# One quarter of M made of 12-bit parts, and a softmax maximum issued ahead of the next rows' parts

## The chip, the cores and the metric

The kernel runs on one core of a Trainium2 chip. The metric is the device time of one execution in microseconds (us), as the median of several runs. Engines are named as the profile names them: PE (TensorE, matmuls), PEld (its weight loads), DVE (VectorE), ACT (ScalarE), POOL (GpSimd) and SP (SyncE). DVE, ACT and POOL each work through one queue of instructions in order; SP and POOL also issue the transfers (DMAs).

## The reference

One decoder layer on x of 4 batches x 512 rows x 512 columns, in float32. The change touches the first of its three blocks, self-attention with 16 heads of 128:

```python
q = x @ Wq + bq ; k = x @ Wk + bk ; v = x @ Wv + bv      # x here: layernorm of the rows
att = softmax(q @ k / sqrt(128))                          # per head: 128 x 128, contracted over the 512 rows
x   = x + (att @ v) @ Wo + bo
x   = x + gamma * cross(layernorm(x), ctx)                # cross-attention, 8 heads
x   = x + ffn(layernorm(x))                               # ternary weights, silu gate
```

## The kernel before, in words

**Work.** The 16 heads go in four quarters j = 0..3 of four heads (512 columns). With the Gram matrix G of the normalized rows of a batch (tiles `xn`, bank `pg`, L444), each quarter of each batch is this chain of 512x512 products: U from the rows and Wo (bank `pu`, tiles `u`), Y from G and Wk (`py`, `y`), M from Wv and U (`pm`, `m`), the scores from Wq and Y (`sc`, L523), a softmax of the scores (maximum `nmax` L531, its scaling L534, exponential on ACT L538, division by the sum L549, result `e`), then, one quarter later, the transpose of `e` (`pe`, L126) and the output product (`po`, L562), which DVE adds to the accumulators `acc` (L564).

**Two kinds of product.** `products_f32` (L384) is 16 float32 matmuls, each of which the profile records as two; ACT copies the four results out. `products` makes the same of parts of 12 bits: each operand is a triple h, l, d. For a pair of result tiles there are 16 matmuls h.h and l.l (L350, L351) into two banks, which ACT copies to tiles of the pool `t` (L357, three buffers), then 8 matmuls d.d (L362) into two other banks; DVE adds both (`total`, L372). Two pairs make one product. `tri_of` makes the parts of a tile: h on ACT (L188), l and d on DVE (L189, L190).

**Which kind where.** Batches 1 to 3 use parts throughout. In batch 0 the weights are loaded raw, and `FIRST` says from which quarter on a product uses parts: 1 for U and Y, 4 (`HG`, so never) for M. `exact(n, b, j)` asks this.

**Weights of batch 0.** `first_weights` loads four raw chunks per weight by SP. For q, k and v it also loads a row `last` by SP, and a bias row into the last line of chunk 3 by a POOL DMA (L265), and DVE folds the two into each chunk (L269). Chunk 3, the one with the bias, is loaded first. `keep_weights` then makes the parts (h on ACT L306, l on DVE L308, and d on DVE only where the quarter is exact) and stores them to DRAM by POOL DMAs (L288), where later batches load them. A part that was not made, batch 1 makes (`weights`, d on DVE L336, stored by POOL L339).

**Order.** PE, DVE and ACT instructions are placed by a scheduler when the kernel is built; `tc.issue_after(mark)` holds a group back until a named instruction has been placed. `mark["copied"]` is the last copy out of a `products` call, `mark["nmax"]` the last softmax maximum. In quarter 3 of batch 0, `normed(1, xs, ...)` normalizes the rows of batch 1 (statistics on DVE L95 and L96, square root on ACT L103, reciprocal L112, four normalizations L120, four one-column memsets L407), and `parts_of(1, xs)` makes their parts (tiles `xh`, `xl`, `xd`). Before a tile that came by DMA is used, `settle` multiplies it by a one (L603, L610) that is made of the newest copied tile (`recent`), which ties it to that point of the order.

**What follows quarter 3 of batch 0.** The Gram matrix of batch 1 (`pg`), the transpose `pe` and output `po` of quarter 3 in its midst, and then quarter 0 of batch 1. Beside batch 1 run as side steps the row norms of batch 0 for the cross-attention (`row_norms`: square root `std_c` on ACT, reciprocal and copy on DVE L112 and L686, a store `norm_a` and two loads `norms` by POOL, L687 and L690), the cross-attention itself (`qs`, `kh` on ACT L723 and L727, `xs` on PE L740), and the bias additions to the new accumulators, which POOL computes (L872).

Of the kernel before, what the change touches and what calls it, by code (L numbers as in the profile page):

```python
# [11 lines left out]
F32 = mybir.dt.float32  # L12

F32R = mybir.dt.float32r
# [5 lines left out]
P = 128  # L20
# [4 lines left out]
NG, HG = 4, 4  # L25
# [14 lines left out]
def decoder_layer_kernel(  # L40
# [169 lines left out]

    FIRST = {"o": 1, "k": 1, "v": HG}

    def exact(n, b, j):
        return b > 0 or j >= FIRST[n]

# [9 lines left out]
    last_rows = {}  # L227

    def last_tile(n, j):
        return first[0].tile([P, GW], F32, tag="last", bufs=3, name=f"{n}_last_{j}")  # L230

    def first_last_rows():

# [38 lines left out]
    def keep_weights(n, j, chunks, first, gate):  # L272


        def part(p, k):
            name = f"{n}_{p}_{j}_{k}"
            if n == "o" and exact(n, 0, j):
                if p != "d":
                    return u3p.tile([P, D], F32R, tag="u3", name=name)
                pool, tag, bufs = first[0], "od", 4  # L280
            elif n == "v":
                pool, tag, bufs = first[0], "vpart", 6
            else:
                pool, tag, bufs = first[1], "part", 12
            return pool.tile([P, GW], F32R, tag=tag, bufs=bufs, name=name)

        def keep(name, tile):
            nc.gpsimd.dma_start(name[ts(k, P), :], tile)  # L288

        def behind(n, k):  # L290

            if n == "v" and "copied" in mark:
                return tc.issue_after(mark["copied"])
            if n == "k" and k >= KC // 2 and "nmax" in mark:
                return tc.issue_after(mark["nmax"])
            return nullcontext()

        tris = []
        for k, t in enumerate(chunks):
            if n == "q":  # L300
                keep(kept_q[j], t)
                continue
            tri = Tri(part("h", k), part("l", k), part("d", k) if exact(n, 0, j) else None)
            h, l = tri.h.bitcast(F32), tri.l.bitcast(F32)
            with behind(n, k):
                nc.scalar.mul(tri.h, t, gate[0])  # L306
                keep(kept[n, j, "h"], h)
                nc.vector.scalar_tensor_tensor(tri.l, h, -S, t, ALU.mult, ALU.add)  # L308
                keep(kept[n, j, "l"], l)
                if tri.d is not None:  # L310
                    nc.vector.tensor_tensor(tri.d, l, h, ALU.subtract)
                    keep(kept[n, j, "d"], tri.d.bitcast(F32))
            tris.append(tri)
        return tris
# [28 lines left out]
    def products(name, lhs, rhs, done, tick):  # L343

        for pair in ((0, 1), (2, 3)):
            ph = {i: bank(f"{name}h_{i}") for i in pair}
            for k in range(4):
                for i in pair:
                    a, c = lhs(k, i), rhs(k)
                    nc.tensor.matmul(ph[i], lhsT=a.h, rhs=c.h, start=(k == 0), stop=False)  # L350
                    nc.tensor.matmul(ph[i], lhsT=a.l, rhs=c.l, start=False, stop=(k == 3))  # L351
                if k == 1:
                    tick()
            hs = {}
            for i in pair:
                hs[i] = tp.tile([P, 512], F32, tag="t", name=f"{name}t_{i}")
                mark["copied"] = nc.scalar.copy(hs[i], ph[i]).ins  # L357
            tick()
            pd = {i: bank(f"{name}d_{i}") for i in pair}
            for k in range(4):  # L360
                for i in pair:
                    nc.tensor.matmul(  # L362
                        pd[i], lhsT=lhs(k, i).d, rhs=rhs(k).d, start=(k == 0), stop=(k == 3)
                    )
            for i in pair:
                done(i, hs[i], pd[i])
            recent[:] = [recent[-1], hs[pair[0]]] if recent else [hs[pair[0]]]
            tick()
# [8 lines left out]
    def products_f32(name, lhs, rhs, done, midway=None):  # L377

        for i in range(4):
            if i == 2 and midway:  # L380
                midway()
            p = bank(f"{name}_{i}")
            for k in range(4):
                nc.tensor.matmul(  # L384
                    p, lhsT=lhs(k)[:, ts(i, P)], rhs=rhs(k), start=(k == 0), stop=(k == 3)
                )
            done(i, p)
# [11 lines left out]
    def normed(b, xs, by_chunk):  # L399

        mv = small.tile([P, NG, 2], F32, tag="mv", name=f"mv_a_{b}")

        def finish(part, std):
            rstd = inverse(std, f"a_{b}_{part[0]}")
            for g in part:
                normalize(xs[g], xs[g], mv[:, g, 0:1], rstd[:, g - part[0] : g - part[0] + 1])
                last = nc.vector.memset(xs[g][:, D - 1 : D], 1.0).ins  # L407
            return last

        parts = [(g,) for g in range(NG)] if by_chunk else [tuple(range(NG))]  # L410
        due = []
        for part in parts:
            for g in part:
                if b > 0:
                    settle(xs[g])
                moments(mv[:, g, :], xs[g], f"a_{b}_{g}")
            if b == 0:
                with tc.issue_after(mark["std"]):
                    nc.scalar.copy(accs[part[0]], xs[part[0]])
            due.append((part, std_of(mv[:, part[0] : part[-1] + 1, :], f"a_{b}_{part[0]}")))  # L420
            if len(due) > 1:
                finish(*due.pop(0))
        return finish(*due.pop())
# [457 lines left out]
    for j in range(HG):  # L881
        us, ys, ms = {}, {}, {}

        def to(tiles, pool, tag, name):
            def done(i, p, d=None):
                tiles[i] = pool.tile([P, 512], F32, tag=tag, name=f"{name}_{i}")
                if d is None:
                    evict(tiles[i], p)
                else:
                    total(tiles[i], p, d)  # L890

            return done

        ticks = [0]

        def third_tick():
            ticks[0] += 1
            if ticks[0] == 3:
                midway()

        def midway():
            if waiting:
                waiting[2] = turned(*waiting[:3])

        w = first_weights("o", j, first, gates["o"])
        if exact("o", 0, j):
            w = keep_weights("o", j, w, first, gates["o"])
            products(
                f"pu_0_{j}", lambda c, m: cols(x3[c], m), lambda c: w[c],
                to(us, u3p, "u3", f"u_0_{j}"), lambda: None,  # L910
            )
        else:
            products_f32(
                f"pu_0_{j}", lambda c: xs[c], lambda c: w[c], to(us, u3p, "u3", f"u_0_{j}")
            )
            if j == 0:
                g3 = gram_rest(0, G)
            with tc.issue_after(rows_done):
                keep_weights("o", j, w, first, gates["o"])
        gates["v"] = gate_of(us[3])  # L920
        w = first_weights("k", j, first, gates["k"])
        done = to(ys, yp, "y", f"y_0_{j}")
        if exact("k", 0, j):
            w = keep_weights("k", j, w, first, gates["k"])
            products(
                f"py_0_{j}", lambda e, m: cols(g3[e], m), lambda e: w[e], done, third_tick
            )
        else:
            products_f32(f"py_0_{j}", lambda e: G[e], lambda e: w[e], done, midway)
            keep_weights("k", j, w, first, gates["k"])  # L930
        gates["o"] = gates["k"] = gates["q"] = gate_of(ys[3])
        if waiting:
            output(*waiting)
        w = first_weights("v", j, first, gates["v"])
        products_f32(f"pm_0_{j}", lambda k: w[k], lambda k: us[k], to(ms, mp, "m", f"m_0_{j}"))
        keep_weights("v", j, w, first, gates["v"])
        w = first_weights("q", j, first, gates["q"])
        e = scores(0, j, w, ys)
        keep_weights("q", j, w, first, gates["q"])
        if j == 0:  # L940
            bo_bc = bias_rows(0)
            load(gam, gamma.to_broadcast([P, 1]))
            biased(accs, bo_bc)
        if j + 1 == FIRST["o"]:
            x3 = parts_of(0, xs)
        if j == HG - 2:
            xs = rows_of(1)
        if j == HG - 1:
            normed(1, xs, False)
            x3 = parts_of(1, xs)  # L950
        waiting = [0, j, e, ms, accs]
    first_pools.close()

# [233 lines left out]
```

## Time and profile before

| | |
|---|---|
| median of 3 runs | 1158.3 us (1157.48 to 1159.26) |
| profiled execution | 1157.7 us; its span in the trace 1155.9 us, so 1.8 us lie around it |
| PE busy | 1144.6 us, 99% of the span |
| DVE, ACT, POOL busy | 818.9 us (71%), 524.5 us (45%), 318.8 us (28%) |
| granted TensorE clock | 9 tenths or more in every slice |
| DMA | 270.16 MB, mean 234 GB/s; 9 tenths busy in many slices of the first half |

Rows of a timeline give the start in the span, the duration, the engine, line, operation, output<-input, the count that the row gathers, and in brackets the idle time before it with what ended it. Durations of neighbouring records of one engine overlap a little, so a distance from start to start is what one more instruction costs.

### The profile page before, as it was taken

The page shows a single profiled execution, that of the slowest core. Times are in us where ns is not written, and L with a number is a line of the kernel's source. Part 1 is how long each engine was busy: PE and PEld are TensorE (multiplying, and loading weights), DVE is VectorE, ACT ScalarE, POOL GpSimd, SP SyncE. Part 2 cuts the span into 40 slices and gives each one's busy share as a digit, 9 for nine tenths or more (in the row PEclk, how much of TensorE's full clock was granted, in tenths as well). Part 3 has the DMA queues.
Part 4 walks back from the last instruction along what each step waited for, and adds up shares of the span by engine and source line. Part 5 has one row for each costly group of instructions (what it writes and reads, how often), then busy time and mean ns, then how long its engine had stood idle before and what let it go on. Part 6 is the DMA issues. An engine that isn't in the chain of part 4 may idle for free.

```text
span 1155.9 us, 16616 instructions
## 1 busy us (share of the span) xinstructions
PE 1144.6 (99%) x5282; PEld 856.5 (74%) x5282; DVE 818.9 (71%) x1802; ACT 524.5 (45%) x1073; POOL 318.8 (28%) x550
## 2 busy tenths in 40 slices
PE   8999999999999999999999999999999999999998
PEld 4486684777777768887786787777778877777886
DVE  6768657979797967869697758787957857536232
ACT  5434334435445443545354434544455768534020
POOL 3355443442232324112321332222112212000000
PEclk9999999999999999999999999999999999999999
DMA  9799996798889769997997699799881422122100
GB/s 327 251 329 322 343 359 231 248 331 279 260 292 332 232 235 323 298 286 249 325 305 253 211 345 295 226 336 320 295 282 58 128 82 64 46 74 73 64 1 37
DMA packets 145137, 270.16 MB, mean 234 GB/s; under 512 B 18252, under 2 KB 48260, under 8 KB 145050
## 3 DMA queue, kind: packets, MB, share of 16 engines
q1 hardware_dynamic: 111162, 164.40, 43.0%
q0 software_dynamic: 33872, 104.70, 26.8%
q8 instruction: 42, 0.69, 0.2%
q14 instruction: 45, 0.37, 0.1%
q10 hardware_dynamic: 16, 0.00, 0.0%
HBM read 206.10 MB, written 62.93 MB: 233 GB/s over the span
## 4 chain that ended last, share of the span: by engine, by line
PE 80%; DMA 2%; DVE 2%; issue 1%; ACT 0%; POOL 0%; DVEq 0%; ACTq 0%; POOLq 0%
PE h L1094 14%; PE y L1129 7%; PE xo L784 5%; PE xp L126 5%; PE po L562 4%; PE sc L523 3%; PE xs L740 2%; PE xs L741 2%; PE pg L444 2%; PE pu_1d L362 1%; PE pu_2h L350 1%; PE pm_2d L362 1%; PE pm_3h L350 1%; PE py_3h L350 1%; PE pm_3d L362 1%; PE pu_2h L351 1%
## 5 line engine op out<-in xcount | busy, mean ns | idle before, releaser
L1094 PE MATMUL h<-fxh,t 128*128 128x512 f32 (+1 forms) x352 | 139.6, 397 | 0.0
L1094 PE MATMUL h<-fxl,t 128*128 128x512 f32 (+1 forms) x352 | 137.4, 390 | 0.0
L751 ACT ACTIVATE p<-xs,xnmax 128x512 f32<-128x512 f32 x128 | 87.2, 689 | 82.9 <-PE xp L126 68.3
L745 DVE TENSOR_REDUCE xnmax<-xs 128x1 f32<-128x512 f32 x128 | 83.5, 684 | 23.9 <-PE xs L741 23.8
L1094 PEld LDWEIGHTS h<-fxh,t 128*128 128x128 f32 (+1 forms) x352 | 65.0, 185 | 15.4 <-issue 1.1
L1094 PEld LDWEIGHTS h<-fxl,t 128*128 128x128 f32 (+1 forms) x352 | 65.0, 185 | 14.7 <-issue 0.2
L1129 PE MATMUL y<-t,gh 128*128 128x512 f32 (+1 forms) x176 | 69.3, 394 | 0.0
L1129 PE MATMUL y<-t,gl 128*128 128x512 f32 (+1 forms) x176 | 68.8, 391 | 0.0
L129 ACT COPY pt<-xp 128x512 f32<-128x512 f32 x96 | 54.1, 595 | 30.7 <-PE xp L126 30.7
L126 PE MATMUL xp<-ident,p 128*128 128x128 f32 x512 | 66.5, 273 | 0.0
L126 PEld LDWEIGHTS xp<-ident,p 128*128 128x128 f32 x512 | 59.3, 140 | 9.4 <-issue 2.4
L703 POOL DMA_DIRECT2D xd<-x_a x64 | 33.8, 533 | 115.1 <-DVE qs L724 93.0
L784 PE MATMUL xo<-pt,vals 128*64 128x512 f32 x256 | 61.5, 599 | 0.0
L1107 DVE SCALAR_TENSOR_TENSOR gf<-h,scales_w,sl 128x512 f32<-128x512 f32 (+1 forms) x44 | 32.9, 747 | 39.7 <-PE h L1094 36.4
L763 DVE TENSOR_SCALAR p<-p,xrden 128x512 f32<-128x512 f32 x128 | 56.9, 487 | 3.0
L562 PE MATMUL po<-m,eT 128*128 128x512 f32 x128 | 58.1, 594 | 0.2 <-DVE y L372 0.2
L1103 ACT ACTIVATE sl<-h,scales_w 128x512 f32<-128x512 f32 (+1 forms) x44 | 30.1, 688 | 58.7 <-PE h L1094 58.5
L384 PE MATMUL pm<-u,v_raw 128*128 128x512 f32 x128 | 55.6, 592 | 0.0
L138 POOL CAST gh<-gf 128x512 fp32r<-128x512 f32 (+1 forms) x24 | 15.8, 660 | 137.2 <-DVE gf L1107 121.1
L740 PE MATMUL xs<-kh,qs 128*128 128x512 f32 x128 | 50.1, 392 | 0.0
L741 PE MATMUL xs<-kl,qs 128*128 128x512 f32 x128 | 50.0, 390 | 0.0
L139 DVE TENSOR_TENSOR gl<-gf,gh 128x512 fp32r<-128x512 f32 (+1 forms) x44 | 30.4, 690 | 25.6 <-POOL gh L138 18.6
(317 smaller groups left out, 2921.9 us busy)
## 6 DMA issues: line engine op xcount, KB each, us to landing
oh<-kept_oh SPq DMA_DIRECT2D x48, 256.0 KB, 6.4
ol<-kept_ol SPq DMA_DIRECT2D x48, 256.0 KB, 6.0
kh<-kept_kh SPq DMA_DIRECT2D x48, 256.0 KB, 5.9
kl<-kept_kl SPq DMA_DIRECT2D x48, 256.0 KB, 5.4
vh<-kept_vh SPq DMA_DIRECT2D x48, 256.0 KB, 6.8
vl<-kept_vl SPq DMA_DIRECT2D x48, 256.0 KB, 6.7
q<-kept_q SPq DMA_DIRECT2D x48, 256.0 KB, 6.3
od<-kept_od SPq DMA_DIRECT2D x44, 256.0 KB, 7.4
```

Source lines behind the costliest of these rows:

```text
L126: nc.tensor.transpose(pt[:, ts(k, P)], src[:, ts(k, P)], ident)
L129: nc.scalar.copy(dst, pv)
L384: nc.tensor.matmul(p, lhsT=lhs(k)[:, ts(i, P)], rhs=rhs(k), start=(k == 0), stop=(k == 3))
L562: nc.tensor.matmul(po, lhsT=eT[:, g, :], rhs=ms[g], start=True, stop=True)
L740: nc.tensor.matmul(sc, lhsT=q[:, ts(m, P)], rhs=kh, start=True, stop=False)
L741: nc.tensor.matmul(sc, lhsT=q[:, ts(m, P)], rhs=kl, start=False, stop=True)
L745: nc.vector.reduce_max(nmax[:, i : i + 1], scs[i], axis=AX.X)
L751: nc.scalar.activation(p, scs[i], AF.Exp, bias=nmax[:, i : i + 1], scale=xscale, accum_out=den[:, i : i + 1],)
L763: nc.vector.tensor_scalar(ps[i], ps[i], rden[:, i : i + 1], None, ALU.mult)
L784: nc.tensor.matmul(po[half, :], lhsT=vals[c][:, l, half], rhs=pt[j][:, l, :], start=(l == 0), stop=(l == NC - 1),)
L1094: nc.tensor.matmul(ph[:r, :], lhsT=t[:, block(i, k)], rhs=fxT[j][:, k, :], start=(k == 0 and j == 0), stop=(k == KC - 1 and j == 1),)
L1129: nc.tensor.matmul(py, lhsT=g[i][j][:r, ts(c, P)], rhs=t2[:r, i, :], start=(i == 0 and j == 0), stop=(i == NHC - 1 and j == 1),)
```

## The change

M of quarter 3 of batch 0 becomes a `products` call. For that the parts of Wv are made before it and include d (stored too); U of that quarter goes to a float32 tile of the pool `t` and from there into parts; the parts of Wv there are held back until the last copy of U (`mark["u"]`) and no longer until that of Y. Two pools change: `last` has two buffers and had three, `vpart` eight and had six, and the d parts of Wv use the four buffers `od`. In the same quarter `normed(1, ...)` is called ahead of `scores`, and the parts of the next rows are held back until `nmax`. Batch 1 then loads these four d parts and no longer makes them.

```diff
-    FIRST = {"o": 1, "k": 1, "v": HG}
+    FIRST = {"o": 1, "k": 1, "v": HG - 1}
...
     def last_tile(n, j):
-        return first[0].tile([P, GW], F32, tag="last", bufs=3, name=f"{n}_last_{j}")
+        return first[0].tile([P, GW], F32, tag="last", bufs=2, name=f"{n}_last_{j}")
...
+            elif n == "v" and p == "d":
+                pool, tag, bufs = first[0], "od", 4
             elif n == "v":
-                pool, tag, bufs = first[0], "vpart", 6
+                pool, tag, bufs = first[0], "vpart", 8
...
             if n == "v" and "copied" in mark:
-                return tc.issue_after(mark["copied"])
+                return tc.issue_after(mark["u"] if exact(n, 0, j) else mark["copied"])
...
+            u3 = {}
+
+            def in_parts(m, h, d):
+                us[m] = tp.tile([P, D], F32, tag="t", name=f"u_0_{j}_{m}")
+                total(us[m], h, d)
+                u3[m] = Tri(
+                    *(u3p.tile([P, D], F32R, tag="u3", name=f"u{p}_0_{j}_{m}") for p in "hld")
+                )
+                tri_of(u3[m], us[m])
+
             products(
                 f"pu_0_{j}", lambda c, m: cols(x3[c], m), lambda c: w[c],
-                to(us, u3p, "u3", f"u_0_{j}"), lambda: None,
+                in_parts if exact("v", 0, j) else to(us, u3p, "u3", f"u_0_{j}"), lambda: None,
             )
+            mark["u"] = mark["copied"]
...
         w = first_weights("v", j, first, gates["v"])
-        products_f32(f"pm_0_{j}", lambda k: w[k], lambda k: us[k], to(ms, mp, "m", f"m_0_{j}"))
-        keep_weights("v", j, w, first, gates["v"])
+        done = to(ms, mp, "m", f"m_0_{j}")
+        if exact("v", 0, j):
+            w = keep_weights("v", j, w, first, gates["v"])
+            products(
+                f"pm_0_{j}", lambda k, g: cols(w[k], g), lambda k: u3[k], done, lambda: None
+            )
+        else:
+            products_f32(f"pm_0_{j}", lambda k: w[k], lambda k: us[k], done)
+            keep_weights("v", j, w, first, gates["v"])
         w = first_weights("q", j, first, gates["q"])
+        if j == HG - 1:
+            normed(1, xs, False)
         e = scores(0, j, w, ys)
...
         if j == HG - 1:
-            normed(1, xs, False)
-            x3 = parts_of(1, xs)
+
+            with tc.issue_after(mark["nmax"]):
+                x3 = parts_of(1, xs)
```

Lines named above are those of the kernel before; from the changed lines on, those of the changed kernel are 2 or more higher.

## The prediction

> **What bounds the kernel now.** I read the page first: one engine is busy for nearly the whole span.
>
> ```profile
> span 1155.9 us, 16616 instructions
> PE 1144.6 (99%) x5282; PEld 856.5 (74%) x5282; DVE 818.9 (71%) x1802; ACT 524.5 (45%) x1073; POOL 318.8 (28%) x550
> ```
>
> PE is idle for 11.3 us in all, so time goes only with PE work or with one of PE's waits. PE's waits, second, say which there are:
>
> ```profile
> PE pe L126 <- DVE e L549: 2.0, 1, 2.0
> PE pm_0d L362 <- DVE vd L336: 0.7, 2, 0.5
> ```
>
> The first, 2.0 us, lies in the changed quarter; the second comes just after it, in quarter 0 of batch 1. PE's timeline, third, prices both kinds of product:
>
> ```profile
> 161.40 0.39 PE L350 MATMUL py_3h<-k_h,gh 128*128 128x512 f32 x1
> ...
> 165.03 1.98 PE L362 MATMUL py_3d<-k_d,gd 128*128 128x512 f32 x8
> 166.85 0.60 PE L126 MATMUL pe<-ident,e 128*128 128x128 f32 x4
> ...
> 172.76 3.84 PE L562 MATMUL po<-m,eT 128*128 128x512 f32 x8
> 176.44 13.90 PE L384 MATMUL pm<-u,v_raw 128*128 128x512 f32 x32
> 190.17 3.73 PE L523 MATMUL sc<-y,q_raw 128*128 128x128 f32 x32
> 193.74 6.18 PE L444 MATMUL pg<-xn 128*128 128x512 f32 x16
> 201.96 0.92 PE L126 MATMUL pe<-ident,e 128*128 128x128 f32 x4 [2.04 <-DVE e L549]
> ```
>
> DVE's timeline, fourth, shows what it does meanwhile. Look at the 7.17 us ahead of the last fold, and at how late `nmax` comes:
>
> ```profile
> 172.35 0.75 DVE L269 SCALAR_TENSOR_TENSOR v_raw<-v_last,gate,v_raw 128x512 f32<-128x512 f32 x1 [7.17 <-issue]
> ...
> 190.42 1.47 DVE L120 TENSOR_SCALAR xn<-xn,mv_a,rstd_a 128x512 f32<-128x512 f32 x3
> 191.37 0.06 DVE L407 MEMSET xn<- 128x1 f32 x1
> ...
> 197.60 0.68 DVE L531 TENSOR_REDUCE nmax<-sc 128x4 f32<-128x512 f32 x1
> 198.31 0.17 DVE L534 TENSOR_SCALAR nmax<-nmax 128x4 f32<-128x4 f32 x1
> ...
> 234.46 4.81 DVE L336 SCALAR_TENSOR_TENSOR vd<-vl,one,vh 128x512 fp32r<-128x512 f32 x4
> ```
>
> POOL's, last:
>
> ```profile
> 164.29 0.52 POOL L265 DMA_DIRECT2D v_raw<-in_bqkv_dram  x1
> ...
> 220.87 0.55 POOL L687 DMA_DIRECT2D norm_a<-mv_c  x1 [1.67 <-DVE mv_c L686]
> 225.86 1.40 POOL L690 DMA_DIRECT2D norms<-norm_a  x2 [4.44 <-DMA norm_a<-mv_c]
> ...
> 232.04 6.01 POOL L872 TENSOR_TENSOR acc<-acc,bo_bc 128x512 f32<-128x512 f32 x4 [1.06 <-DVE one L603]
> ```
>
> The bias row of Wv was issued at 164.29 and the fold that needs it began at 172.35, after an idle stretch: 8.06 us for 2 KB. The order of instructions that I use below is that of the two programs as built; the durations are those of these rows.
>
> **Part by part.** All within the profiled execution: span 1155.9, time 1157.7, which is 0.6 below the median of 1158.3; the sum is a difference and is set on the median.
>
> 1. *M of quarter 3 in parts.* It takes 190.17 - 176.44 = 13.73 now. In parts a pair costs what a pair of `py_3` costs: 165.03 - 161.40 = 3.63 for 16 matmuls, 166.85 - 165.03 = 1.82 for 8. Two pairs: 10.90. **-2.83.**
>
> 2. *The parts of Wv come before M, and the last one is late.* DVE now makes, after the bias fold: l and d of chunks 0 to 2, then `y_2`, `y_3`, the four `acc` with a gate between, then l of chunk 3. The fold's pitch is 173.02 - 172.35 = 0.67 (the next row starts at 173.02). From 173.02: three pairs of l and d are 4.0 (from l to l, the parts of Wk before it stand 1.33 apart, 148.64 to 149.97), two y 1.2, four acc 2.4 and the gate 0.2: 180.8, and 0.7 for the l itself, 181.5. PE needs it as the 14th matmul of the first pair, at 176.44 + 13 x 0.227 = 179.4. **+2.1.** All of it hangs on when the bias row lands: 2 us earlier and it is 0; more transfers stand ahead of it now (a load of `last` waits for the folds of another weight, since there are two buffers), so up to 1.3 later, +3.4, is my upper bound. d of chunk 3 follows l by two instructions (1.3) and is due 2.1 after it, so it adds nothing. The parts of U are 8 DVE instructions, 4.9 us, in the 4.15 and 7.17 us where DVE idled; without that cover they would push the folds by up to 4.9. The four extra d of Wv are in the 4.0 and 1.3 above; their stores on POOL are behind everything that PE waits for here. Scores then start at 176.44 + 10.90 + 2.1 = 189.4, 0.7 early.
>
> 3. *`nmax` ahead of the normalization.* In the built order DVE does `nmax`, its scaling, reciprocal, `xn_0`, `xn_1`, then the first memset, which the Gram matrix waits for. From the rows: 0.71 (197.60 to 198.31), two small ones 0.2 each, 0.95 from first `xn` to first memset (190.42 to 191.37), 0.06 and some 0.1 for the hand-over: 2.3 after the scores' end, where now the Gram matrix follows the scores at once. The statistics don't make it worse: they now hang on the copy of M's third bank (some 188.1 by the sum) and end near 192.6, before the scores do. **+2.3.** `pg` at 189.4 + 3.57 + 2.3 = 195.3, against 193.74: 1.6 late. ACT's Sqrt and Exp tables are loaded during this time.
>
> 4. *The wait for `e` goes.* `nmax` at 193.2 rather than 197.60, so `e` is ready some 4 us earlier, near 198, and PE reaches `pe` near 201.3. **-2.04**, and the transposes themselves run 0.36 to the next instruction (166.85 to 167.21, the transposes of the quarter before) rather than 0.75: **-0.3.** Late next on DVE are the eight `xl`, `xd`, 5.3 us, now between `e` and the Gram parts. They fill the 2.91 us in which DVE waited for ACT and the 0.79 us ahead of the `acc`; first needed at 210, they are done by 207.
>
> Up to quarter 0 of batch 1: -2.83 + 2.1 + 2.3 - 2.04 - 0.3 = **-0.8**, and by the start times the same (`pg` 1.6 late, then -2.04 and -0.3).
>
> 5. *Given back at `vd`.* In quarter 0 of batch 1 PE waits 0.7 for the d parts of Wv, which DVE makes from 234.46. DVE has the same work up to there and no gap left to catch up in, so PE arriving early waits longer. On the other side, the settling of `norms` no longer stands ahead of them. Instead the reciprocal of the row norms does, behind `std_c`, which ACT now does after the four copies of `py_0` (ended near 232.0): 1.28 for the table and 0.30 put it at 233.6 and the first `vd` near 234.1. **+0.4**, from 0 to 1.2.
>
> [...] This trace shows 1.28 for the load at 218.25 and `std_c` at 219.54, so no drain. [...]
>
> 6. *Row norms later.* `norm_a` is stored near 234 rather than 220.87, and the loads of `norms` now stand on POOL behind the four additions (6.01) and a store of `vd`: issued near 234.1 + 0.55 + 6.01 + 0.54 = 241.2, landed near 245.7 if they take the 4.4 us that the store took. `kh` and `qs` on ACT (238.69 and 239.32 now) wait for that and hold the copies of M's second pair (243.28 now) by some 4 us; DVE holds `m_2`, `m_3` and the next `nmax` (249.12 now, near 250.3 then). PE has other work there: Scores at 245.35 and U of quarter 1 at 248.8. **+0.3**, from 0 (that cover holds) to 2.1 (it doesn't).
>
> 7. *Batch 1, quarter 3.* Four DVE instructions and four stores go, four loads of 256 KB come, with no PE wait at that place: 0, between -0.3 and +0.3.
>
> Sum: -0.8 + 0.4 + 0.3 + 0 = -0.1, on the median **1158.2**.
>
> [...] The row says 8.06 us, in a window where the DMA engines are nine tenths busy, so I go by the row.
>
> **The rivals.**
>
> *Faster (the gains stay).* If the bias row lands 2 us earlier, because the reordered loads drain sooner, step 2 is 0 and the sum -2.2; if `vd` and the norms cost nothing too, -2.9: 1155.4 to 1156.1. For: the stall of 2.04 is the largest in this part and surely goes. Against: 8.06 us, with full DMA slices around it.
>
> *Slower (the row norms decide).* If the 4 us hold of ACT's copies reaches a bank that PE needs, PE stands for up to 2.1 in quarter 0 or 1 of batch 1, and with a bias row 1.3 later the sum is -0.1 + 1.8 + 1.3 = +3.0: 1161.3. It decides once `norms` lands after some 247.5, when the third copy of `pm_0` comes after U of quarter 1 wants its banks. For: two queue positions on POOL worse, 6 us of additions ahead. Against: scores and U run without those tiles.
>
> *It doesn't do what it says.* The scheduler could have left `nmax` behind the parts; in the built program it doesn't, so I give this no part of its own.
>
> **How the numbers follow.** About 0.2% (2.3 us) can be told from no change. The forecast, the gains eaten by the l part, the Gram matrix's wait and `vd`, within 2.3 of 1158.3: 0.44. Faster by more, 1156.0 or less: 0.23. Slower, 1160.6 or more: 0.33, above the other since three of the open costs (bias row, `vd`, norms) have their longer side there. The range, 1155.5 (bias row early, nothing given back) to 1161.5 (the slower rival), leaves out 0.2.
>
> **What would show it.** Right: two pairs of `pm_3` at 3.63 and 1.82 with one wait of about 2 us on `v_l` inside the first; `pg` waiting about 2.3 us on DVE; no wait before `pe`; a wait of 0.7 to 1.5 on `vd`; `norms` loaded after the additions. Wrong: no wait on `v_l` (time near 1156), or PE waiting on ACT's copies of `pm_0` or for a bank after 245 (time above 1160).

## The result, and the profile after

| | before | after |
|---|---|---|
| median | 1158.48 us (1156.51 to 1160.79) | 1161.39 us (1157.09 to 1163.66) |
| ratio | 1 | 1.0026, 95% interval 1.0018 to 1.0034 |
| profiled execution | 1157.7 us, span 1155.9 | 1160.1 us, span 1158.3 |

The changed kernel is slower by 0.26%, some 3 us. The time lies inside the range and just above the bound that the prediction gave to its slower cases; the forecast was 1158.2. The page after, first part:

```profile
span 1158.3 us, 16683 instructions
PE 1141.6 (99%) x5298; PEld 858.7 (74%) x5298; DVE 827.0 (71%) x1813; ACT 527.1 (46%) x1077; POOL 316.7 (27%) x550
```

PE has 3.0 us less to do (1144.6 before), and the span is 2.4 us longer: all of the loss is waiting. The waits of PE after (total, times, longest):

```profile
PE pm_0d L364 <- DVE vd L338: 4.1, 1, 4.1
...
PE pg L446 <- DVE xn L409: 2.2, 1, 2.2
PE py_0d L364 <- DMA kd<-kept_kd: 1.0, 2, 0.8
...
PE xs L743 <- DVE kl L730: 0.6, 1, 0.6
```

The wait of `pe` is gone and that of `pg` is there, as forecast; the wait on `v_l` that the forecast had is missing. The one on `vd`, 0.7 before, has become the longest of this part. PE's timeline after:

```profile
187.44 3.73 PE L525 MATMUL sc<-y,q_raw 128*128 128x128 f32 x32
193.39 6.25 PE L446 MATMUL pg<-xn 128*128 128x512 f32 x16 [2.22 <-DVE xn L409]
199.47 0.60 PE L126 MATMUL pe<-ident,e 128*128 128x128 f32 x4
199.91 2.78 PE L446 MATMUL pg<-xn 128*128 128x256 f32 x16
...
206.32 0.47 PE L352 MATMUL pu_0h<-oh,xh 128*128 128x512 f32 x1
...
236.43 0.50 PE L364 MATMUL pm_0d<-ud,vd 128*128 128x512 f32 x1 [4.12 <-DVE vd L338]
```

The scores start at 187.44, against 190.17; U of quarter 0 of batch 1 at 206.32, against 210.78. So PE is 4.5 us ahead of the kernel before when batch 1 begins. All of it is gone at one place, the `vd` wait. DVE and POOL there:

```profile
230.00 6.38 DVE L338 SCALAR_TENSOR_TENSOR vd<-vl,one,vh 128x512 fp32r<-128x512 f32 x2
```

```profile
230.32 0.54 POOL L689 DMA_DIRECT2D norm_a<-mv_c  x1 [0.80 <-DVE bo_bc L612]
230.88 4.94 POOL L874 TENSOR_TENSOR acc<-acc,bo_bc 128x512 f32<-128x512 f32 x4
...
236.43 0.72 POOL L692 DMA_DIRECT2D norms<-norm_a  x1
```

Two `vd` in 6.38 us: the first takes 0.75, as always; the second begins at 230.66, 0.22 ahead of POOL's four additions, and ends at 236.38, 0.56 behind the last of them. It takes 5.7 us for 0.75 us of work. In the kernel before the same four `vd` fell into the midst of the additions; two of them took 1.78 and 1.77, the others 0.74. The two long ones, before:

```profile
235.12 3.48 DVE L336 SCALAR_TENSOR_TENSOR vd<-vl,one,vh 128x512 fp32r<-128x512 f32 x2
```

Note too where `norms` is loaded: behind the additions, as forecast.

Where the end's 2.67 us come from, by the starts of PE's stages, after minus before (us):

| stage | difference |
|---|---|
| scores of quarter 3, batch 0 | -2.7 |
| Gram matrix, second part (ahead of it `pe`) | -2.5 at `pe` |
| U of batch 1, quarter 0 | -4.5 |
| M of that quarter | -4.45 |
| scores of that quarter | +0.1 |
| scores of quarter 1 | -0.5 |
| M of batch 2, quarter 0 | +1.6 |
| start of the feed-forward block | +1.6 |
| the same, behind the `xs` at 886.8 (after) in its midst | +2.5 |
| end | +2.7 |

So the hold takes the lead and no more: from the scores of quarter 0 to the end of batch 1 the two kernels are within 0.5 us of each other. The 3.1 us by which the changed kernel falls behind come later, in batch 2 and in the feed-forward block.

From -2.5 to -4.5 there is no wait. It is the clock. The windows of 3 us give the length, then PE, PEld, DVE, ACT and POOL busy with counts, then the granted clock, the DMA share and GB/s; before, in the second part of the Gram matrix:

```profile
204.00:207.00 3.00, 3.00 (x14) 2.62 (x13) 2.97 (x6) 0.37 (x1) 1.86 (x4) 0.54 0.38 147
```

and after, in the same work, and behind the `vd` wait:

```profile
199.00:202.00 3.00, 3.00 (x18) 2.48 (x18) 3.00 (x6) 1.71 (x4) 0.00 (x0) 1.00 0.00 0
...
237.00:240.00 3.00, 3.00 (x9) 2.32 (x8) 2.30 (x8) 1.64 (x3) 3.00 (x6) 0.52 0.55 183
```

In each kernel one stretch of 3.41 us runs at half clock (granted 0.50): before, from 203.34, behind the 2.04 us stall of `pe`, which made the second part of `pg` take 4.28 rather than 2.62; after, from 237.10, behind the stall of 4.12.

### The profile page after: what moved, and what is told of

Its sections match the earlier page's. It is cut to its first block, busy times and chain, and to the rows that moved or that the text cites. A ratio compares the mean times of both kernels' runs of the same rounds, so it can differ in the third digit from the quotient of the medians.

```text
span 1158.3 us, 16683 instructions
## 1 busy us (share of the span) xinstructions
PE 1141.6 (99%) x5298; PEld 858.7 (74%) x5298; DVE 827.0 (71%) x1813; ACT 527.1 (46%) x1077; POOL 316.7 (27%) x550
## 4 chain that ended last, share of the span: by engine, by line
PE 93%; DMA 3%; issue 2%; DVE 1%; POOL 0%; ACT 0%; ACTq 0%; DVEq 0%; POOLq 0%
PE h L1117 12%; PE y L1152 7%; PE sc L525 5%; PE xo L786 5%; PE xp L126 5%; PE po L564 4%; PE pm L386 4%; PE pg L446 3%; PE xs L743 3%; PE xs L742 3%; PE pu_1d L364 1%; PE pu_2h L352 1%; PE pm_3h L352 1%; PE pu_1h L353 1%; PE py_3h L352 1%
## 5 line engine op out<-in xcount | busy, mean ns | idle before, releaser
L188 ACT ACTIVATE uh<-u 128x512 fp32r<-128x512 f32 x52 | 33.0, 634 | 34.6 <-DVE u L374 34.6
```

## The experiments

The theory going in: the front's gain is real, and DVE's `vd`, held by POOL's additions, gives it away. The rivals: M in parts costs it (the late `v_l`, fewer `last` buffers), or the late row norms do. Ratios are to the kernel before on the same chip, with 95% intervals; all ten kernels compute the whole layer.

One fact of the built programs has to stand first. The changed kernel without its second edit (`normed` behind the scores, no hold on the parts) is built into the same instructions in the same order on PE, DVE, ACT, POOL and SP. With M in parts the scheduler puts the maximum first by itself. So the difference measured above is that of M in parts alone, order included.

### The additions behind M of quarter 0

In the changed kernel (`adds_behind`) and in the kernel before (`before_adds_behind`), POOL's four additions go to where no `vd` is due:

```diff
-        settle(bo_bc)
...
-        return biased(accs, bo_bc)
+        return accs
...
+            if j == 0:
+                settle(bo_bc)
+                biased(accs, bo_bc)
             e = scores(...)
```

> The changed kernel; only the settling of the bias tile and the four POOL additions to the accumulators of batches 1 to 3 come later, after M of quarter 0 (PE, ACT and SP keep their order). Theory 1 (POOL's additions hold DVE: in the changed kernel one vd took 5.7 us while four additions ran without a gap, and PE waited 4.1 us for it): that vd takes 0.75, PE's wait at pm_0d falls from 4.1 to 1 or less, scores of quarter 0 start near 242, and the time is 3 to 4.5 us below the changed kernel's 1161.4: 1157.0 to 1158.4, so 0 to 1.5 under before. Theory 2 (the loss is in what follows 250 us: late loads of batch 2, row norms, cross-attention; the wait at vd only takes the gain back): the time stays at 1160.5 to 1162. Theory 3 (vd is late because DVE has too much to do, not because of POOL): the wait stays at 3 to 4 and the time at 1161.

> The same move of the four POOL additions in the kernel before. Theory 1: its vd instructions, two of which took 1.78 us beside two additions, take 0.75; PE's wait of 0.7 goes; time 0.5 to 1 us below before, 1157.5 to 1158.0. Theories 2 and 3: no change, 1158.5.

Measured: 1.0042 (1.0025 to 1.006) and 0.9985 (0.9972 to 0.9998). The first is a miss: the `vd` wait went, the scores came at -3.2, and the time rose. The lines of PE's waits, DVE and POOL of `adds_behind` say why:

```profile
PE pu_1h L352 <- ACT e L540: 4.5, 1, 4.5
```

```profile
251.27 3.96 DVE L536 TENSOR_SCALAR nmax<-nmax 128x4 f32<-128x4 f32 x1
```

```profile
250.20 4.99 POOL L873 TENSOR_TENSOR acc<-acc,bo_bc 128x512 f32<-128x512 f32 x4
```

The hold has only moved. Now the scaling of `nmax`, 0.17 us of work on 128x4, stands for 3.96 us until the last addition ends at 255.19; `e` waits for it, and PE for `e`. In the kernel before no DVE instruction fell into the additions, and the move gave a little. How much of it is the `vd` is not shown: that trace has a stall of only 1.2 at `pe`, against 2.04, ahead of the place that was changed, and a mean granted clock of 0.999, against 0.998.

### The second edit alone

`order_only` is the kernel before with `normed` ahead of the scores and the parts held for `nmax`, M in float32 as before:

```diff
+        if j == HG - 1:
+            normed(1, xs, False)
         e = scores(0, j, w, ys)
...
-            normed(1, xs, False)
-            x3 = parts_of(1, xs)
+            with tc.issue_after(mark["nmax"]):
+                x3 = parts_of(1, xs)
```

> The kernel before with the second edit alone: normed(1) ahead of scores(0, 3) and the next rows' parts held back until nmax; M of quarter 3 stays float32. As built, nmax follows the normalizations and memsets but precedes the parts xl, xd. Theory 1: the wait of 2.0 us before pe goes, the Gram matrix is not delayed (193.7), so PE reaches quarter 0 of batch 1 some 2.3 us early; how much survives is decided at vd, where the additions stand: wait 0.7 plus up to 2.3 there, time 1156.5 to 1159. Theory 2: the gain stays until 250 us and later losses don't come, since no loads are added: 1156.0 to 1156.5.

Measured: 0.9979 (0.9967 to 0.999), 2.4 us faster. Without M in parts the edit does move instructions. The `pe` wait is gone, the mean granted clock is 0.999 against 0.998, and U of batch 1 starts 2.6 us earlier. The hold is there as well:

```profile
237.54 3.92 DVE L610 TENSOR_TENSOR abs_w<-abs_w,one 128x1 f32<-128x1 f32 x1
```

```profile
237.66 3.77 POOL L872 TENSOR_TENSOR acc<-acc,bo_bc 128x512 f32<-128x512 f32 x3
```

An instruction on 128x1 takes 3.9 us, but little waits for it: PE's wait on `vd` is 1.4 in all.

### Three buffers for `last`

The changed kernel with `bufs=2` of the tag `last` set back:

```diff
-        return first[0].tile([P, GW], F32, tag="last", bufs=2, name=f"{n}_last_{j}")
+        return first[0].tile([P, GW], F32, tag="last", bufs=3, name=f"{n}_last_{j}")
```

> The changed kernel with three buffers for the rows called last, as before, not two. The bias row of Wv landed at 169.7 in the changed kernel and at 172.3 before. If the changed order of loads is what brought it early, it lands near 172 here and PE waits about 2 us on v_l inside pm_3, as predicted; by theory 1 the wait at vd then shrinks by as much (4.1 to 2) and the time stays near 1161. If the order of loads has nothing to do with it, there is no wait on v_l and nothing changes: 1161. By theory 2 the 2 us come on top: 1163.

Measured: 1.0031 (1.0014 to 1.0047): nothing comes back. PE's waits:

```profile
PE pm_0d L364 <- DVE vd L338: 4.1, 1, 4.1
...
PE pm_3h L353 <- DVE v_l L310: 2.1, 1, 2.1
```

The wait on `v_l` that the changed kernel's trace lacks is 2.1 here, as expected if the order of loads matters. The bias row took 8.4 us from its issue to its landing; with two buffers it took 6.4 to 7.4 (the five other traces with M in parts), and with three and M in float32 7.6 to 8.2 (six traces). So two buffers go with a row that lands about 1 us sooner, where the prediction had it later. They do not decide alone: with two buffers the wait on `v_l` still goes from 0 to 1.8.

The `vd` wait did not shrink, as was expected of theory 1. PE began M of quarter 0 3.6 us later than in the changed kernel and waited 4.1 again, with 5.71 us in the second `vd`: the store, the additions and the `vd` had moved along with PE. So this wait is not made by PE coming early.

### The additions on DVE

To end the hold rather than move it, the additions go to DVE at the same later place: `after_dve`, `before_dve`, and `order_dve` (on `order_only`).

```diff
-    def biased(accs, bo_bc):
+    def biased(accs, bo_bc, engine=nc.gpsimd):
...
-            nc.gpsimd.tensor_tensor(acc, acc, bo_bc, ALU.add)
+            engine.tensor_tensor(acc, acc, bo_bc, ALU.add)
...
+            if j == 0:
+                settle(bo_bc)
+                biased(accs, bo_bc, nc.vector)
```

> The changed kernel with the sixteen-less-four bias additions of batches 1 to 3 (four in each) done by DVE ahead of the maximum of quarter 0, where it waited 2.5 us for the scores, and none by POOL. So far: beside POOL's four additions one DVE instruction was held until the last of them ended (a vd for 5.7 us in the changed kernel, the scaling of a maximum for 4.0 us when the additions stood behind M). Theory 1 (the hold is what took the gain back): no DVE instruction over 1.3 us between 200 and 1160, no wait of over 1 us on vd or e; PE is some 3 us ahead of before at the scores of quarter 0 and stays so: time 3 to 4.5 below the changed kernel, 1157 to 1158, with a remainder of 1 to 2.5 lost after 400 (kd of batch 2, cross-attention in the FFN). Theory 3 (DVE has too much to do): four more instructions on DVE make it worse, 1161 to 1164.

> The same move of the additions to DVE in the kernel before. Theory 1: the two vd of 1.78 us take 0.75, PE's wait of 0.7 on vd goes, nothing else changes: 0.7 to 1.5 below before, like the kernel whose POOL additions came later (ratio 0.9985). Theory 3: slower than before by up to 2.

> The second edit alone (normed ahead of scores, parts of the next rows held back until the maximum; ratio 0.9979 to before) with the additions on DVE. Theory 1: its vd of 1.8 us and a settling step held for 3.9 us go, PE's wait of 1.4 on vd goes: 1 to 1.5 below that kernel, ratio to before 0.9965 to 0.997, the fastest of all. Theory 3: slower than the second edit alone.

Measured: 1.0024 (1.001 to 1.0038), 0.999 (0.9977 to 1.0003), 0.9971 (0.9959 to 0.9983). In the traces of `after_dve` and `before_dve` no DVE instruction takes over 1.3 us any more, and the `vd` wait is gone from both. The ratios of `before_dve` and `order_dve` can't be told from those of the kernels that they start from. And `after_dve` is as slow as the changed kernel: a miss, and the one that showed the second cause. ACT, then PE, of `after_dve`:

```profile
245.98 0.72 ACT L729 ACTIVATE kh<-kd,norms 128x512 fp32r<-128x512 f32 x1 [9.82 <-DMA norms<-norm_a]
```

```profile
248.33 0.50 PE L742 MATMUL xs<-kh,qs 128*128 128x512 f32 x1 [1.08 <-DVE qs L726]
...
256.72 0.79 PE L352 MATMUL pu_1h<-oh,xh 128*128 128x512 f32 x1 [3.10 <-ACT e L540]
```

ACT stands 9.82 us before `kh` because the row norms land only then; the copies of M and `e` stand behind it in ACT's queue, and PE loses 4.2 us. The 4 us that the hold had cost are now lost to the norms. `adds_behind` has this too: there ACT stood 9.43 us before `kh`, ahead of the held scaling.

The norms themselves are later than in the changed kernel: the last of them lands at 245.76, there at 239.36. The two loads of 4 KB took 6.1 and 6.2 us, there 2.4 and 2.2. From 235 to 240 us the DMA engines were busy to 1.02 here and to 0.46 there, where PE and DVE had just stood still.

### The row norms early

The side step `row_norms` is issued whole, right behind the last output of batch 0, instead of a piece at a time:

```diff
-            itertools.chain(row_norms(b - 1, waiting[4]), cross(b - 1, *cpool)),
+            itertools.chain([None] * len([*row_norms(b - 1, waiting[4])]), cross(b - 1, *cpool)),
```

`after_norms` is the changed kernel with this, `after_dve_norms` has the additions on DVE too, and `order_dve_norms` is the last without M in parts.

> The changed kernel with the row norms of the batch before (statistics, std_c, store, loads) queued whole, right behind the output that makes the rows, not spread as side steps; the four POOL additions stay where they were. As built, std_c stands ahead of the copies of U and the norms are loaded ahead of the kd stores. Theory 1 (POOL's additions hold one vd for 5 us) alone: the hold stays, unless the additions and the vd now miss each other; PE's wait at vd 2.5 to 4 and the time 1159.5 to 1161. Theory 4 (two things in a row take the gain: the held vd, and behind it the late norms, which hold ACT's copies of M and with them the next maximum): the same here, since the held vd is still first in the row: 1159.5 to 1161.

> Both: the bias additions on DVE (no POOL addition beside vd) and the row norms queued early. With the additions on DVE alone the wait at vd was gone, but norms landed at 246, ACT and DVE stood for them, and PE waited 1.1 for qs and 3.1 for e. Theory 4: both waits are gone, no wait of over 1 us between 200 and 300; PE passes the scores of quarter 1 some 3 us ahead of before; after 400 up to 2.7 may be lost as in the other kernels with M in parts (kd of batch 2 about 1.6, cross-attention in the FFN 0.9): time 1155 to 1157.5, ratio to before 0.9975 to 0.9995. If the late norms are not what made e late: the wait of 3.1 stays and the time is 1160.

> The second edit alone with both moves (additions on DVE, norms early). With the additions on DVE this kernel had ratio 0.9971 and waits of 0.8 on vd and 2.1 on a load of od at 254. Theory 4: norms were not late there, so nothing or up to 1 us is gained: ratio 0.9962 to 0.9975.

Measured: 1.0004 (0.9995 to 1.0013), 0.9972 (0.9963 to 0.9981) and 0.9963 (0.9949 to 0.9977); the last, 1153.69 us, is the fastest of all. `after_norms` did better than expected. The norms are loaded at 219.6, and DVE now comes to `vd` when the additions already run:

```profile
232.18 5.86 DVE L338 SCALAR_TENSOR_TENSOR vd<-vl,one,vh 128x512 fp32r<-128x512 f32 x4
```

Three of these four take about 1.8 us, each waiting for one addition only, and PE's wait is 2.2 rather than 4.1. So this edit changes the hold as well as the norms. What is left of PE's waits in this part in `after_dve_norms`:

```profile
PE pg L446 <- DVE xn L409: 2.2, 1, 2.2
...
PE pm_3h L353 <- DVE v_l L310: 0.7, 1, 0.7
PE pm_0d L364 <- DVE vd L338: 0.5, 1, 0.5
```

The four kernels with M in parts, ratios to the kernel before:

| | norms late | norms early |
|---|---|---|
| additions on POOL | 1.0026 | 1.0004 |
| additions on DVE | 1.0024 | 0.9972 |

With the norms late, ending the hold is worth nothing that can be told; with the norms early it is worth 0.0032, some 3.7 us, and with the additions on DVE the early norms are worth 0.0052, some 6 us. The intervals of each of these last two pairs lie apart. So the loss has two causes in a row, and the gain comes only when both are taken away. With the additions on POOL the early norms are worth 0.0022, but they shortened the hold too.

Not all of the 6 us is the 4.2 of PE's waits on late norms. Between the traces of `after_dve` and `after_dve_norms` there go also 1.0 of wait on `kd` in batch 2, 1.1 of the wait on `v_l`, and the time at half clock: the mean granted clock is 1.0 in `after_dve_norms`, 0.998 in `after_dve` and `after_norms`, and 0.999 in the changed kernel.

`order_dve_norms` and `after_dve_norms` overlap: when nothing gives it back, M in parts is worth nothing that can be told beyond the order alone. In the trace of `after_dve_norms` the waits at `pg` and `v_l` are 2.9 together, near the 3 us that the products save.

## Why the prediction was right or wrong

**Step 1, right.** `po` and M together take 14.33 (173.11 to 187.44) against 17.41: -3.1, forecast -2.83.

**Step 2, too large, and not steady.** The fold that needs the bias row began at 169.67, not 172.35:

```profile
169.67 0.75 DVE L269 SCALAR_TENSOR_TENSOR v_raw<-v_last,gate,v_raw 128x512 f32<-128x512 f32 x1 [0.58 <-DMA v_raw<-in_bqkv_dram]
```

The row took 6.6 us from its issue at 163.05, and PE waited for no `v_l`. Over the six kernels with M in parts the wait was 0, 0.3, 0.7, 1.5, 1.8 and 2.1, a mean of 1.1. The forecast took the upper of these as its value, and had the two buffers on the wrong side: the 2.1 is the kernel with three.

**Step 3, right.** 2.22 at `pg`, forecast 2.3; the terms written there add up to 2.22.

**Step 4, right but for a term.** The wait of 2.04 went and the transposes took 0.44 rather than 0.75: -0.31, as the sum had it, though its own two rows (0.36 and 0.75) give -0.39. The sum had no place for what the stall had cost after its end, the half clock: 4.28 - 2.62 = 1.7 us. The front as a whole came to -4.8 (39.12 from the transposes of the quarter before to U of batch 1, against 43.93), where the sum said -0.8; nearly all of the difference is this term and the `v_l` that did not come late.

**Step 5, the step that failed.** +0.4, at most 1.2, for the `vd`; measured +4.5 from M's start to the scores: 3.4 of wait above the 0.7 of before, and the rest with the half clock behind it. The working moved the start of the `vd` to 234.1 and left the row as it was before, 4.81 for four. It did not ask how that row was made: two of its four were already twice as long as a `vd` needs, because POOL's additions ran beside them. Step 6 starts the additions near 234.7 rather than 232.04, so the working had them move against the `vd`, and it priced that at nothing. Nor is it PE's early arrival that made the wait: in `last3` PE came 3.6 us later and waited as long.

**Step 6, right in mechanism, too small in size, and hidden.** In the changed kernel the norms landed at 239.36, not near 245.7, about when `kh` had begun in the kernel before (239.32), and PE waited for nothing behind them; +0.3 was near. Where nothing was held (`after_dve`), they landed at 245.76, and PE lost 4.2 us; the bound was 2.1.

**Step 7 and later, missing in the sum.** Batch 1 lost nothing more: at its end the changed kernel was at -0.5, the sum at -0.1. That is luck, since the front was 4.0 better than its forecast and the `vd` 4.1 worse. Then batch 2 gave +2.1, nearly all of it in the product that waits 1.0 for the loads of `kd`, and the `xs` of the last cross-attention, inside the feed-forward block, +0.9, of which 0.6 is a wait on `kl`. The first wait stands in four of the six kernels with M in parts (1.0 to 1.3) and not in the two with early norms; `order_only` has late norms and only 0.2 of it. The second stands in all six and in none without, with another DVE order there. Neither was in the sum, which ended at batch 1, and what makes these loads and `kl` late is left open. So the hold is why no gain was left, and these later terms are why the trace ends behind.

**The rivals.** The slower one named the row norms. They did not decide in the changed kernel, and came to cost 4.2 us once the hold was gone. That its price of 1161.3 is near the measured 1161.4 is luck: other terms made up the sum. The third, that the change does not do what it says, was dismissed on the order of the built program, which is as the change asks; but that order comes without the second edit. Building the first edit alone would have told this beforehand.

## What to carry to other kernels

A wait that goes is worth more than its length if the clock drops behind it (here 2.04 us, and 1.7 behind them), and PE's lead is worth nothing until the next place that waits for a slower engine has been asked what it will meet there. When two engines hold each other up, a duration read from a row of before is one phase of a collision (four `vd` in 4.81 us here, and 5.72 for one of them after), so read the single records and ask how the row moves against the other engine's. And an edit that only asks a scheduler for an order should be built alone first: here the edit was empty beside its companion and, taken by itself, was the faster kernel.

## What the runs showed of the hardware

**The hold.** Beside POOL's additions (1.25 to 1.30 us each when nothing stands in between) some DVE instructions, all on SBUF operands, were held, in two ways. In one the instruction waited for a single addition and the engines then alternated: 1.78 and 1.77 us for a `vd` of 0.74 (before, 235.12 and 236.83), and about 1.8 in `after_norms`. In the other it began 0.12 to 0.22 us ahead of an addition with more behind it, and was held until the last had ended: 5.72 (`vd` in the changed kernel) and 5.71 (`vd` in `last3`), with four to come, 3.96 (the 128x4 scaling in `adds_behind`, three to come) and 3.92 (the 128x1 product in `order_only`, three). The distance does not decide alone: a `vd` that began 0.09 us ahead of an addition took 0.74, and POOL was the one held, with 1.81 for its addition (before, 234.46), and one that began 0.02 ahead waited for one addition only (`after_norms`, 232.18). Others were not held. Beside the addition that began at 250.20 in `adds_behind`, the second of two sums on DVE that read PSUM was not lengthened (249.36, the usual 1.27 for both), and a maximum that reads PSUM took its usual 0.68 (250.55); beside the one that began at 230.96 in `after_norms`, a reduction of one SBUF tile took its usual 0.68 (`sums_w`, 230.86).

Why a hold goes on through three or four additions is not settled; the pattern stands in four traces.

**The clock.** A stall of 2.04 us (before) was followed by 3.41 us at a granted clock of 0.50, one of 4.12 (after) as well, and one of 2.22 (`pg`, after) by none. Both stretches lie on a grid of 3.41 us that is counted from the clock's first record some 12 us into the span: before, from 12.19 to 203.34, are 56 times 3.413, and after, from 11.82 to 237.10, 66 times. On this grid the stalls differ. The window that holds the 2.04, before, with PE busy for 1.38:

```profile
199.93:203.34 3.41, 1.38 (x7) 1.16 (x8) 1.91 (x9) 3.34 (x12) 0.00 (x0) 1.00 0.00 0
```

and the first of the two that share the 2.22, after, with PE busy for 1.86 (2.74 in the second):

```profile
189.31:192.72 3.41, 1.86 (x17) 1.67 (x15) 2.86 (x11) 0.84 (x2) 0.83 (x2) 1.00 0.32 129
```

In these two traces, from that first record to the last matmul, two windows of this grid were followed by half clock, those in which PE idled for 2.03 us (before) and 2.74 (after, 233.69 to 237.10). None of the others was; the longest idle times among them are 1.55, 1.37 and 1.05, all after. So the idle time within one window goes with the drop here, not the length of a stall; from these figures the limit is, by estimate, between 1.55 and 2.03 of the 3.41. The times agree: the kernel before took 1160.5 us on average in the 11 runs of one chip with a mean granted clock of 0.998 or less, and 1156.9 in the 19 above.
